# Graph attention stack on one core: outer products and aggregation of the last layer as one piece, in column tiles; one operation less in each norm

## The chip, the cores and the metric

The kernel runs on one core of a Trainium2 chip. It is a single program. The metric is the device time in microseconds (us) from the first to the last instruction; the time before is the median of three runs. A core has a matrix engine (TensorE, in the profile PE, its weight loads PEld), a vector engine (VectorE, DVE), an activation engine (ScalarE, ACT), a general engine (GpSimd, POOL) and a queue that starts transfers (SyncE, SP). Each has its own stream of instructions in fixed order, and they wait for one another through semaphores.

## The reference

There are 16 batches of 1024 nodes with 128 features. Three layers of masked attention with 8 heads and a feed-forward part come first; the fourth and last layer is a graph attention with one score per pair of nodes. All share one adjacency matrix.

```python
# layers 0 to 2
Q, K, V = h @ Wq, h @ Wk, h @ Wv                    # 8 heads of 16
scores  = where(adj == 0, -inf, Q K^T / sqrt(16))
attn    = softmax(scores) @ V
x = layer_norm(h + (attn @ Wo + bo))
x = layer_norm(x + relu(x @ W1 + b1) @ W2 + b2)

# layer 3, the last
h   = x @ W
e   = (h @ a_src)[:, :, None] + (h @ a_dst)[:, None, :]
e   = where(e >= 0, e, 0.2 * e)
e   = where(adj == 0, -inf, e)
att = softmax(e)
y   = einsum('bij,bjd->bid', att, h) + x
out = ln_gamma * (y - mean(y)) * rsqrt(var(y) + 1e-5) + ln_beta
```

In the last layer the exponential of a leaky sum of two terms is the larger of two products, one for each slope. So the kernel builds the numerators as outer products of two vectors, with no exponential per pair of nodes: TensorE forms a ratio as an outer product, VectorE takes the maximum with 1 and multiplies by the mask. The rest is in factors per node.

## The kernel before

The kernel is one long loop over score steps: 48 blocks (16 batches, 3 layers) of 32 steps. Each step makes scores for four heads (128 keys, 512 queries) on TensorE, exponentials and masks on the other three engines, and the weighted sum (attention times values) of the step that is four steps older. After the weighted sum of a step one *piece* of other work may be put in: a transpose, a projection, a part of the feed-forward layer, a part of the last layer. The pieces stand in chains, and a piece has a smallest distance in steps from the one before it.

```python
for at, (g, qh, kt) in enumerate(...):              # the steps of a block
    ...
    e = score_step(step)                            # L395 scores; L402, L403, L405, L417 on the other engines
    waiting.append((step, e, n + AHEAD))            # AHEAD = 4
    av_due(n)                                       # L422: weighted sum of an older step
    piece()                                         # at most one piece of other work
    n += 1

def piece():
    for chain in chains:
        if now[0] >= chain["due"] + chain["queue"][0][0] and take(chain):
            return
```

TensorE and ScalarE keep the order in which the program was written. The scores go to three pairs of banks of PSUM (`slot`), two in each step; all pieces share one bank (`bank`); tiles for the exponentials are six, and the outer products take from the same six.

```python
def slot(dtype=F32):
    return psum.tile([P, N], dtype, tag="s", name="s", bufs=3)
def bank():
    return psum.tile([P, 512], F32, tag="t", name="t", bufs=1)
def e_tile():
    return work.tile([P, J, 512], F32, tag="e", name="e", bufs=6)
```

A helper splits a matmul with 128 output rows into four, each with 32 columns of the weights and 32 output rows. The projections and the feed-forward part use it (L271):

```python
def by_columns(dst, lhsT, rhs, start=True, stop=True):
    for j in range(0, P, SLOT):                     # SLOT = 32
        nc.tensor.matmul(dst[j:j + SLOT, :], lhsT[:, j:j + SLOT], rhs, start=start, stop=stop)
```

The norms take mean and variance from VectorE and finish on GpSimd:

```python
def normalise(n, ts):
    z, _, mv = n
    m, v = mv[:, ts, 0], mv[:, ts, 1]
    nc.gpsimd.tensor_scalar(m, m, -1.0, None, op0=OP.mult)                   # L311
    nc.gpsimd.tensor_scalar(v, v, EPS, None, op0=OP.add)                     # L312
    nc.gpsimd.tensor_tensor(v, v, half_neg[:, ts], OP.pow)                   # L313
    for t in range(ts.start, ts.stop):
        nc.gpsimd.tensor_scalar(z[:, t, :], z[:, t, :], mv[:, t, 0:1], mv[:, t, 1:2], op0=OP.add, op1=OP.mult)   # L315
```

The last layer of a batch is a chain of pieces. A batch has four units of 256 queries; each unit has outer products and an aggregation:

```python
def nodes(t0, t1):                                  # projection of the nodes, L539
    ...
        nc.tensor.matmul(ps[:, (t - t0) * (D + 2):(t - t0 + 1) * (D + 2)],
                         s["xT", t // 4][:, t % 4 * P:(t % 4 + 1) * P], w_nodes, start=True, stop=True)
    ...
def edges(u):                                       # outer products of unit u
    e = s["e", u] = e_tile()...
    for c in range(2):
        ps = slot()
        ...  nc.tensor.matmul(ps[...], h_rows[...], g_rows[...], start=True, stop=True)          # L579, four
        nc.vector.scalar_tensor_tensor(e[:, c:NT:2, :], ps..., 1.0, mask01[...], op0=OP.max, op1=OP.mult)   # L582
def aggregate(u):
    e, ps = s["e", u], bank()
    for i in range(2):
        for t in range(NT):                         # NT = 8
            nc.tensor.matmul(ps[:, i * (D + 1):(i + 1) * (D + 1)], e[:, t, i * P:(i + 1) * P],
                             s["hd"][t // 4][:, t % 4, :], start=(t == 0), stop=(t == NT - 1))   # L591
    nc.vector.reciprocal(s["col"][:, 3, 2 * u:2 * u + 2], pv[:, :, D])                           # L594
    ...  # L597: times the reciprocal, plus x; then the statistics; a norm after every second unit

return [..., (2, rows_gh, ""), (8, edges(0), ""), (2, edges(1), ""), (1, aggregate(0), ""),
        (2, edges(2), ""), (1, aggregate(1), ""), (2, edges(3), ""), (1, aggregate(2), ""),
        (2, aggregate(3), ""), (4, end, "-x -last -w -w")]
```

The first number of an entry is the smallest distance in steps; the strings name tiles that the piece takes or gives back.

Of the kernel before, what the change touches and what calls it, by code (L numbers as in the profile page):

```python
# [15 lines left out]
OP = mybir.AluOpType  # L16
AX = mybir.AxisListType

P = 128
# [87 lines left out]
def fast_path(ctx: ExitStack, tc: tile.TileContext, a: dict, out: bass.AP, flag):  # L107
    nc = tc.nc
    x_dram, adj = a["x"], a["adj"]
    B, N, D = x_dram.shape  # L110
    NT = N // P
# [13 lines left out]
    def bank():  # L125

        return psum.tile([P, 512], F32, tag="t", name="t", bufs=1)
# [80 lines left out]
    w_nodes = const.tile([P, D + 2], F32)  # L208
# [36 lines left out]
    for i in range(2):  # L245
        t = const.tile([P, NT, H, HD + 1], F32, name=f"v{i}")
# [4 lines left out]
    def soon():  # L251

        return tc.high_priority(offset=SOON)
# [14 lines left out]
    def by_columns(dst, lhsT, rhs, start=True, stop=True):  # L268

        for j in range(0, P, SLOT):  # L270
            nc.tensor.matmul(dst[j:j + SLOT, :], lhsT[:, j:j + SLOT], rhs, start=start, stop=stop)  # L271
# [16 lines left out]
    def with_stats(x):  # L288

        return (x, work.tile([P, NT, 6], F32, tag="st", name="st", bufs=4),  # L290
                work.tile([P, NT, 2], F32, tag="mv", name="mv", bufs=4))
# [15 lines left out]
    def normalise(n, ts):  # L307

        z, _, mv = n
        m, v = mv[:, ts, 0], mv[:, ts, 1]  # L310
        nc.gpsimd.tensor_scalar(m, m, -1.0, None, op0=OP.mult)  # L311
        nc.gpsimd.tensor_scalar(v, v, EPS, None, op0=OP.add)  # L312
        nc.gpsimd.tensor_tensor(v, v, half_neg[:, ts], OP.pow)  # L313
        for t in range(ts.start, ts.stop):
            nc.gpsimd.tensor_scalar(z[:, t, :], z[:, t, :], mv[:, t, 0:1], mv[:, t, 1:2], op0=OP.add, op1=OP.mult)  # L315

    def scale_shift(z, gain, bias):
        n = z.shape[1]
        nc.gpsimd.tensor_mul(z, z, rows(gain, n))  # L319
        nc.gpsimd.tensor_add(z, z, rows(bias, n))  # L320
# [192 lines left out]
    def last_tasks(b):  # L513
        s = {}
        g0 = 32 * (b % 2)

        def xt(h):
            def run():
                w = W[L - 1]
                if h == 0:  # L520

                    s["col"] = work.tile([P, 4, NT], F32, tag="col", name="col", bufs=2)
                    s["hd"] = [work.tile([P, 4, D + 1], F32, tag="w", name="hd", bufs=TILES["w"]) for _ in range(2)]
                    s["n"] = with_stats(state["x", b])
                s["xT", h] = transpose_half("xT", state["x", b], h, w["ln2_gc"], w["ln2_bc"])
                if h == 1:
                    scale_shift(state["x", b], w["ln2_g"], ln2_b_last)
            return run

        def nodes(t0, t1):  # L530
            def run():
                col, ts = s["col"], slice(t0, t1)

                halves = [slice(max(t0, 4 * h), min(t1, 4 * h + 4)) for h in range(2)]
                halves = [(c, s["hd"][c.start // 4][:, c.start % 4:(c.stop - 1) % 4 + 1, :])
                          for c in halves if c.start < c.stop]
                ps = bank()
                for t in range(t0, t1):
                    nc.tensor.matmul(ps[:, (t - t0) * (D + 2):(t - t0 + 1) * (D + 2)],  # L539
                                     s["xT", t // 4][:, t % 4 * P:(t % 4 + 1) * P], w_nodes, start=True, stop=True)  # L540
                pv = ps[:, :(t1 - t0) * (D + 2)].rearrange("p (t d) -> p t d", d=D + 2)
                with soon():
                    nc.scalar.activation(col[:, 2, ts], pv[:, :, D + 1], AF.Exp, scale=NEG_SLOPE)
                    nc.scalar.activation(col[:, 0:2, ts].rearrange("p c t -> p t c"), pv[:, :, D:], AF.Exp,
                                         scale=1 - NEG_SLOPE)
                    for c, hd in halves:
                        nc.vector.tensor_mul(hd[:, :, :D], pv[:, c.start - t0:c.stop - t0, :D],
                                             col[:, 2, c, None].to_broadcast([P, c.stop - c.start, D]))
                for c, hd in halves:
                    nc.scalar.copy(hd[:, :, D], col[:, 2, c])  # L550
            return run

        def rows_gh():
            ps = bank()[:2 * NT, :P]
            nc.tensor.transpose(ps, s["col"][:, 0:2, :].rearrange("p c t -> p (c t)"), identf)
            parts = work.tile([2 * NT, 2, P], F32R, tag="parts", name="parts", bufs=1)
            with soon():
                nc.scalar.copy(parts[:, 0, :], ps)
                nc.vector.tensor_sub(parts[:, 1, :], ps, parts[:, 0, :].bitcast(F32))
            for r in range(2):  # L560

                queue = nc.scalar if r and b == B - 1 else nc.sync
                for i in range(4):
                    row = 64 * r + g0 + i
                    queue.dma_start(g_rows[row:row + 1, :].bitcast(F32), parts[:NT, i // 2, :].bitcast(F32))
                    queue.dma_start(h_rows[row:row + 1, :].bitcast(F32),
                                    parts[NT + 4 * r:NT + 4 * r + 4, i % 2, :].bitcast(F32))


        def edges(u):  # L570
            def run():
                e = s["e", u] = e_tile().rearrange("p j (c q) -> p (j c) q", q=256)
# [4 lines that stand above are left out]
                        for r in range(2):  # L577
                            row = slice(64 * r + g0, 64 * r + g0 + 4)
                            nc.tensor.matmul(ps[:, (2 * r + i) * 256:(2 * r + i + 1) * 256],  # L579
                                             h_rows[row, (2 * i + c) * P:(2 * i + c + 1) * P],  # L580
                                             g_rows[row, u * 256:(u + 1) * 256], start=True, stop=True)
                    nc.vector.scalar_tensor_tensor(e[:, c:NT:2, :], ps.rearrange("p (j q) -> p j q", q=256), 1.0,  # L582
                                                   mask01[:, c:NT:2, u * 256:(u + 1) * 256], op0=OP.max, op1=OP.mult)
            return run

        def aggregate(u):
            def run():
                e, ps = s["e", u], bank()
                for i in range(2):
                    for t in range(NT):  # L590
                        nc.tensor.matmul(ps[:, i * (D + 1):(i + 1) * (D + 1)], e[:, t, i * P:(i + 1) * P],  # L591
                                         s["hd"][t // 4][:, t % 4, :], start=(t == 0), stop=(t == NT - 1))
                pv = ps[:, :2 * (D + 1)].rearrange("p (i d) -> p i d", d=D + 1)
                nc.vector.reciprocal(s["col"][:, 3, 2 * u:2 * u + 2], pv[:, :, D])  # L594
                for i in range(2):
                    t = 2 * u + i
                    nc.vector.scalar_tensor_tensor(s["n"][0][:, t, :], pv[:, i, :D], s["col"][:, 3, t:t + 1],  # L597
                                                   state["x", b][:, t, :], op0=OP.mult, op1=OP.add)
                stats(s["n"], slice(2 * u, 2 * u + 2))
                if u % 2:  # L600
                    normalise(s["n"], slice(2 * u - 2, 2 * u + 2))
                if u == 3:
                    check_range(s["col"].rearrange("p c t -> p (c t)"))
            return run

        def end():
            y = s["n"][0]
            for h in range(2):
                scale_shift(y[:, 4 * h:4 * h + 4, :], wl["ln_gamma"], wl["ln_beta"])
                queue = nc.scalar if h and b == B - 1 else nc.sync  # L610
                queue.dma_start(out[b].rearrange("(t p) d -> p t d", p=P)[:, 4 * h:4 * h + 4], y[:, 4 * h:4 * h + 4, :])

        return [(5, xt(0), "+w +last +w +w"), (1, xt(1), "+w"), (2, nodes(0, 3), ""), (2, nodes(3, 6), ""), (2, nodes(6, 8), "-w -w"),
                (2, rows_gh, ""), (8, edges(0), ""), (2, edges(1), ""), (1, aggregate(0), ""),
                (2, edges(2), ""), (1, aggregate(1), ""), (2, edges(3), ""), (1, aggregate(2), ""),
                (2, aggregate(3), ""), (4, end, "-x -last -w -w")]

# [94 lines left out]
    with tc.manual_schedule(engines={mybir.EngineType.PE, mybir.EngineType.Activation}):  # L714
        for m, (b, l) in enumerate(blocks):
# [3 lines left out]
            for at, (g, qh, kt) in enumerate((g, qh, kt) for g, qh in order for kt in range(NT)):  # L719
# [18 lines left out]
                e = score_step(step)  # L738
# [23 lines left out]
    ps = bank()  # L762
# [226 lines left out]
```

## Time and profile before

| what | value |
|---|---|
| time, median of 3 runs | 4240.29 us (4239.9 to 4240.64) |
| profiled execution, span | 4233.0 us |
| TensorE busy | 3878.9 us (92%) |
| VectorE busy | 3405.0 us (80%) |
| ScalarE busy | 3396.3 us (80%) |
| GpSimd busy | 3449.9 us (82%) |
| scores L395 | 6144 matmul records, 1227.4 us busy |
| weighted sums L422 | 12288 matmul records, 1640.6 us busy |
| aggregation L591 | 2048 matmul records, 267.4 us busy |
| node projection L539 | 256 matmul records, 44.5 us busy |
| VectorE waiting for L591 | 185.7 us, 64 times |
| mean granted TensorE clock | 0.976 |

Busy time of an engine is the union of its instructions, and that of TensorE holds matmuls that overlap. A line of the groups reads: line, engine, operation, output <- input with shape, number; then busy time, mean duration in nanoseconds, and the idle time of that engine just before. A line of the chain that ended last names the piece of work that released the next; at its end it gives by engine 48% TensorE, 22% VectorE, 11% ScalarE, 9% GpSimd and 9% in which nothing shown was waited for. A float32 matmul leaves two records and two weight loads in the trace.

### The profile page before, as it was taken

How to read it: one execution, taken by the hardware profiler on the slowest of the kernel's cores; microseconds unless marked ns; L12 is line 12 of the kernel's file. 1: busy time of each engine (PE TensorE's matmuls, PEld its weight loads, DVE VectorE, ACT ScalarE, POOL GpSimd, SP SyncE). 2: the span in 40 equal slices, each digit the busy share in tenths (PEclk: the TensorE clock that was granted, in tenths of full speed). 3: DMA queues.
4: the chain of work that ended last, by engine and by line, in shares of the span. 5: the costliest groups of instructions: out<-in, count | busy, mean ns of one | idle time of the engine just before them, and what ended most of it. 6: DMA issues, size and time to landing. Idle time of an engine off the chain costs nothing.

```text
span 4233.0 us, 93837 instructions
## 1 busy us (share of the span) xinstructions
PE 3878.9 (92%) x37589; PEld 1582.0 (37%) x37589; DVE 3405.0 (80%) x5324; ACT 3396.3 (80%) x3961; POOL 3449.9 (82%) x3010
## 2 busy tenths in 40 slices
PE   7999999999988999999989999999998899999986
PEld 2333333344443333334444333333444433333445
DVE  6888888877768888888777888888877788888874
ACT  7899999976768999987766899997876689999760
POOL 5888888977769888888766988888886698888785
PEclk9999999999999999999999999999999999999998
DMA  5222122211111222121111212221211212212100
GB/s 150 64 61 61 49 53 61 61 51 51 44 51 49 61 61 61 49 53 51 51 51 51 61 50 52 61 61 43 70 48 36 64 42 61 58 49 57 46 22 17
DMA packets 126235, 232.23 MB, mean 55 GB/s; under 512 B 36704, under 2 KB 75616, under 8 KB 125792
## 3 DMA queue, kind: packets, MB, share of 16 engines
q1 hardware_dynamic: 122896, 225.14, 21.1%
q8 instruction: 299, 4.90, 0.5%
q10 hardware_dynamic: 2896, 1.01, 0.1%
q14 instruction: 144, 1.18, 0.1%
HBM read 15.54 MB, written 8.39 MB: 6 GB/s over the span
## 4 chain that ended last, share of the span: by engine, by line
PE 48%; DVE 22%; ACT 11%; POOL 9%; issue 9%; SPq 1%; DMA 1%; DVEq 0%; ACTq 0%; POOLq 0%
PE acc L422 15%; PE t L271 12%; PE s L395 11%; DVE e L405 11%; PE t L591 6%; POOL e L403 5%; ACT e L417 5%; ACT e L402 4%; DVE st L296 2%; PE t L260 2%; DVE e L582 2%; DVE lo L360 2%; DVE x L303 1%; POOL x L315 1%; DVE tt L433 1%
## 5 line engine op out<-in xcount | busy, mean ns | idle before, releaser
L405 DVE TENSOR_TENSOR e<-s,mask_add 128x1024 f32<-128x1024 f32 x2112 | 2501.3, 1212 | 427.0 <-PE s L395 307.1
L417 ACT ACTIVATE e<-e 128x1024 f32<-128x1024 f32 x2112 | 2196.3, 1063 | 387.4 <-DVE e L405 369.5
L403 POOL TENSOR_TENSOR e<-e,mask 128x1024 f32<-128x1024 f32 x960 | 2049.4, 2152 | 473.9 <-ACT e L402 469.7
L422 PE MATMUL acc<-e,v 128*17 128x512 f32 x12288 | 1640.6, 606 | 73.8 <-POOL e L403 40.9
L395 PE MATMUL s<-Wq,Wk 64*128 64x512 f32 x6144 | 1227.4, 462 | 114.4 <-DVE e L405 37.6
L402 ACT ACTIVATE e<-s 128x1024 f32<-128x1024 f32 x960 | 983.8, 1025 | 272.3 <-PE s L395 169.8
L395 PEld LDWEIGHTS s<-Wq,Wk 64*128 64x128 f32 x6144 | 504.8, 186 | 1087.1 <-DVE e L405 432.4
L422 PEld LDWEIGHTS acc<-e,v 128*17 128x17 f32 x12288 | 207.4, 95 | 584.9 <-issue 459.5
L315 POOL TENSOR_SCALAR x<-x,mv 128x128 f32<-128x128 f32 x896 | 392.1, 453 | 24.1
L591 PE MATMUL t<-hd,e 128*128 128x129 f32 x2048 | 267.4, 292 | 22.3 <-DVE lo L360 17.0
L591 PEld LDWEIGHTS t<-hd,e 128*128 128x128 f32 x2048 | 255.6, 206 | 81.9 <-issue 53.7
L319 POOL TENSOR_TENSOR x<-x,ln_g 128x1024 f32<-128x1024 f32 (+1 forms) x97 | 229.6, 2367 | 30.1 <-PE t L260 29.7
L313 POOL TENSOR_TENSOR mv<-mv,half_neg 128x4 f32<-128x4 f32 x224 | 232.3, 1037 | 18.3
L303 DVE TENSOR_TENSOR x<-t,x 128x512 f32<-128x512 f32 x192 | 131.8, 687 | 102.7 <-PE t L271 101.7
L271 PE MATMUL t<-x1T,W 128*32 128x512 f32 x1536 | 200.8, 594 | 3.4 <-DVE x L597 1.0
L296 DVE BATCH_NORM_STATS2 st<-x 128x6 f32<-128x128 f32 x896 | 196.8, 279 | 2.9
L271 PEld LDWEIGHTS t<-W,hT 128*32 128x32 f32 x6144 | 171.2, 110 | 70.5 <-issue 32.6
L271 PE MATMUL t<-W,hT 128*32 128x128 f32 x6144 | 186.3, 273 | 7.9 <-DVE x L303 3.7
L260 PE MATMUL t<-identf,x 128*128 128x128 f32 x896 | 149.6, 291 | 42.7 <-DVE lo L360 21.6
L260 PEld LDWEIGHTS t<-identf,x 128*128 128x128 f32 x896 | 96.3, 143 | 236.5 <-issue 89.5
L311 POOL TENSOR_SCALAR mv<-mv 128x4 f32<-128x4 f32 x224 | 53.0, 237 | 153.5 <-DVE mv L298 112.1
L594 DVE RECIPROCAL col<-t 128x2 f32<-128x2 f32 x64 | 10.9, 170 | 185.7 <-PE t L591 185.7
(83 smaller groups left out, 2634.3 us busy)
## 6 DMA issues: line engine op xcount, KB each, us to landing
Wk<-hi SPq DMA_DIRECT2D x384, 128.0 KB
Wk<-lo SPq DMA_DIRECT2D x384, 128.0 KB
Wq<-hi SPq DMA_DIRECT2D x384, 128.0 KB
Wq<-lo SPq DMA_DIRECT2D x384, 128.0 KB
x<-in_x_dram SPq DMA_DIRECT2D x16, 512.0 KB
out_dram<-x SPq DMA_DIRECT2D x31, 256.0 KB
ai<-in_adj_dram SPq DMA_DIRECT2D x8, 512.0 KB
g_rows<-parts SPq DMA_DIRECT2D x124, 4.0 KB
```

What stands on the lines that cost most here:

```text
L260: nc.tensor.transpose(ps[:, t * P:(t + 1) * P], src[:, 4 * h + t, :], identf)
L271: nc.tensor.matmul(dst[j:j + SLOT, :], lhsT[:, j:j + SLOT], rhs, start=start, stop=stop)
L296: nc.vector.bn_stats(st[:, t, :], z[:, t, :])
L313: nc.gpsimd.tensor_tensor(v, v, half_neg[:, ts], OP.pow)
L315: nc.gpsimd.tensor_scalar(z[:, t, :], z[:, t, :], mv[:, t, 0:1], mv[:, t, 1:2], op0=OP.add, op1=OP.mult)
L395: nc.tensor.matmul(ps[:, r * 512:(r + 1) * 512], k[64 * r:64 * r + 64, kt * P:(kt + 1) * P], q[64 * r:64 * r + 64, q0:q0 + 512], start=Tru ...
L402: nc.scalar.activation(ev, psv, AF.Exp, scale=HD ** -0.5)
L403: nc.gpsimd.tensor_mul(ev, ev, m)
L405: nc.vector.tensor_add(ev, psv, m)
L417: nc.scalar.activation(ev, ev, AF.Exp, scale=HD ** -0.5)
L422: nc.tensor.matmul(acc[j * SLOT:j * SLOT + HD + 1, :], v_bufs[m % 2][:, kt, 2 * j + g, :], e[:, j, :], start=first, stop=last)
L591: nc.tensor.matmul(ps[:, i * (D + 1):(i + 1) * (D + 1)], e[:, t, i * P:(i + 1) * P], s["hd"][t // 4][:, t % 4, :], start=(t == 0), stop=(t ...
```

## The change

It has three parts, all of which leave the computed function as it is. The outer products of unit u + 1 and the aggregation of unit u become one piece, with a distance of three steps to the next. The aggregation and the node projection are written with the helper for column tiles, four matmuls with 32 columns in place of one with 128; the weighted sums around them work in such tiles too. The norms no longer negate the mean before adding it, but subtract it. The aim is to spare TensorE a change of layout, to let VectorE work on the outer products while TensorE aggregates, and to relieve GpSimd.

```diff
     def normalise(n, ts):
 
         z, _, mv = n
-        m, v = mv[:, ts, 0], mv[:, ts, 1]
-        nc.gpsimd.tensor_scalar(m, m, -1.0, None, op0=OP.mult)
+        v = mv[:, ts, 1]
         nc.gpsimd.tensor_scalar(v, v, EPS, None, op0=OP.add)
         nc.gpsimd.tensor_tensor(v, v, half_neg[:, ts], OP.pow)
         for t in range(ts.start, ts.stop):
-            nc.gpsimd.tensor_scalar(z[:, t, :], z[:, t, :], mv[:, t, 0:1], mv[:, t, 1:2], op0=OP.add, op1=OP.mult)
+            nc.gpsimd.tensor_scalar(z[:, t, :], z[:, t, :], mv[:, t, 0:1], mv[:, t, 1:2], op0=OP.subtract, op1=OP.mult)
 ...
                 for t in range(t0, t1):
-                    nc.tensor.matmul(ps[:, (t - t0) * (D + 2):(t - t0 + 1) * (D + 2)],
-                                     s["xT", t // 4][:, t % 4 * P:(t % 4 + 1) * P], w_nodes, start=True, stop=True)
+                    by_columns(ps[:, (t - t0) * (D + 2):(t - t0 + 1) * (D + 2)],
+                               s["xT", t // 4][:, t % 4 * P:(t % 4 + 1) * P], w_nodes)
 ...
                     for t in range(NT):
-                        nc.tensor.matmul(ps[:, i * (D + 1):(i + 1) * (D + 1)], e[:, t, i * P:(i + 1) * P],
-                                         s["hd"][t // 4][:, t % 4, :], start=(t == 0), stop=(t == NT - 1))
+                        by_columns(ps[:, i * (D + 1):(i + 1) * (D + 1)], e[:, t, i * P:(i + 1) * P],
+                                   s["hd"][t // 4][:, t % 4, :], start=(t == 0), stop=(t == NT - 1))
 ...
+        def two(f, g):
+            def run():
+                f()
+                g()
+            return run
+
         return [...
-                (2, rows_gh, ""), (8, edges(0), ""), (2, edges(1), ""), (1, aggregate(0), ""),
-                (2, edges(2), ""), (1, aggregate(1), ""), (2, edges(3), ""), (1, aggregate(2), ""),
-                (2, aggregate(3), ""), (4, end, "-x -last -w -w")]
+                (2, rows_gh, ""), (8, edges(0), ""), (3, two(edges(1), aggregate(0)), ""),
+                (3, two(edges(2), aggregate(1)), ""), (3, two(edges(3), aggregate(2)), ""),
+                (3, aggregate(3), ""), (4, end, "-x -last -w -w")]
```

## The prediction

> **What bounds the kernel now.** I read the table of engines first: TensorE 92% busy, the other three 80 to 82%. No engine is at its limit over the whole span, and overlapping matmuls are counted as busy, so 92% says little. Next came the busy time by stretch, which shows that the span alternates between two stages:
>
> ```profile
> core 0: us, PE busy (x) PEld busy (x) DVE busy (x) ACT busy (x) POOL busy (x), PEclk, DMA share, GB/s
> 1270.00:1850.00 580.00, 541.71 (x5528) 196.96 (x5526) 491.93 (x752) 519.11 (x591) 518.83 (x449) 1.00 0.23 57
> 1850.00:2320.00 470.00, 431.09 (x3948) 197.71 (x3944) 360.84 (x588) 331.07 (x402) 347.76 (x303) 0.95 0.19 50
> ```
>
> The first row has no last layer in it: ScalarE and GpSimd are busy 89% of it. The second has the last layer of four batches, and ScalarE falls to 70%, GpSimd to 74%. All that the change touches on TensorE is in such stages, where the other engines wait. Who waits is in the timeline of one unit (outer products L579, then aggregation L591), first TensorE; start and duration in us lead each line, the wait before it stands in brackets:
>
> ```profile
> 859.43 1.05 PE L422 MATMUL acc<-e,v 128*17 128x512 f32 x8
> 860.41 0.50 PE L579 MATMUL s<-g_rows,h_rows 4*128 4x256 f32 x4
> 861.33 0.50 PE L579 MATMUL s<-g_rows,h_rows 4*128 4x256 f32 x4 [0.41 <-DVE e L405]
> 861.75 0.49 PE L395 MATMUL s<-Wq,Wk 64*128 64x512 f32 x2
> 862.46 0.50 PE L395 MATMUL s<-Wq,Wk 64*128 64x512 f32 x2 [0.21 <-DVE e L582]
> 862.89 1.05 PE L422 MATMUL acc<-e,v 128*17 128x512 f32 x8
> 863.87 3.84 PE L591 MATMUL t<-hd,e 128*128 128x129 f32 x32
> 867.64 0.73 PE L395 MATMUL s<-Wq,Wk 64*128 64x512 f32 x4
> 868.30 1.05 PE L422 MATMUL acc<-e,v 128*17 128x512 f32 x8
> ```
>
> The same stretch on VectorE:
>
> ```profile
> 861.19 2.35 DVE L582 SCALAR_TENSOR_TENSOR e<-s,mask 128x1024 f32<-128x1024 f32 x2
> 864.08 1.23 DVE L405 TENSOR_TENSOR e<-s,mask_add 128x1024 f32<-128x1024 f32 x1 [0.55 <-PE acc L422]
> 867.75 0.17 DVE L594 RECIPROCAL col<-t 128x2 f32<-128x2 f32 x1 [2.44 <-PE t L591]
> ```
>
> A step of the pipeline goes from one L422 to the next. The step with the outer products takes 3.46 us here, the one with the aggregation 5.41. In the first, TensorE waits for VectorE to empty the score banks; in the second, VectorE waits 2.44 us for the aggregation. The chain that ended last follows the same turns:
>
> ```profile
> 861.19 1.23 DVE e L582
> 862.41 0.04 issue
> 862.46 0.50 PE s L395 x2
> 862.96 0.98 PE acc L422 x8
> 863.94 3.78 PE t L591 x32
> ```
>
> So outer product, score step and aggregation stand one after the other in the time. I measured all steps of the timeline in this way: 491 with nothing between take 1.92 us in the mean, 55 with outer products 3.94, 54 with an aggregation 6.23; together 941 + 217 + 336 = 1,495 us. The other steps carry projections or transposes, and the last ten aggregations lie in the tail after the last score.
>
> [...]from the start of an L422 group, which works in column tiles, to a full-array group takes 0.98 us (862.89 to 863.87), to another group in column tiles 0.87 us (4086.95 to 4087.82). [...]a 32-record group in column tiles goes from 512.55 to the next group at 513.56 (1.01 us), a 64-record one from 4087.82 to 4089.68 (1.86 us), so 26.6 ns for each further record. [...] The stage with the last layer has a mean clock of 0.95 and the other 1.00, and several aggregations take 5.2 to 5.7 us in place of 3.84. [...]here an operation on 4 elements per partition takes 237 ns.
>
> **The change part by part.**
>
> Aggregation in column tiles. The page counts 32 records for 16 matmuls, two for each. Now there are 64 matmuls, so 128 records: 1.86 + 64 x 0.0266 = 3.56 us to the next group, where the full array takes 3.77 (863.87 to 867.64). With 0.11 us less for entering, an aggregation saves 0.32 us. Four tiles side by side do not make it four times as fast[...]. This is an estimate from groups with 128 moving columns, here it is 129.
>
> One piece instead of two. The order of the two built programs on TensorE gives: 42 steps with both (outer products of the next unit, then the aggregation of this one), 14 with outer products alone, 13 with an aggregation alone, and 529 empty in place of 490 (the timeline shows one more). The combined step, from the lines above: first outer products at +0.98, second at +1.90 (still behind L405), +0.42 until the next group can start, 3.56 for the aggregation, 0.66 for the scores: 6.5 us. VectorE's 2.35 us on the outer products now lie beside the aggregation, and its wait shrinks from 2.44 to about 1.8 us (861.19 + 2.35 = 863.54, against 859.43 + 5.9 = 865.3). But the two steps measured are dearer in the mean than the clean case: 3.94 - 3.46 = 0.5 and 6.23 - 5.41 = 0.8. [...] I give the combined step half of this 1.3: 7.2 us. The sum: 42 x 7.2 + 14 x 3.94 + 13 x 5.9 + 529 x 1.92 = 302 + 55 + 77 + 1,016 = 1,450, or 45 us less. With none of the excess it would be 73 less, with all of it 18.
>
> Node projections in column tiles. Six full records go from 4057.09 to 4057.96 (0.87 us); 24 records in tiles are 0.19 + 24 x 0.0266 = 0.83, and 0.11 for entering: 0.15 us saved, with four records 0.13. For 28 and 14 steps: 6 us.
>
> Norms. The negation on GpSimd goes, 224 times:
>
> ```profile
> L311 POOL TENSOR_SCALAR mv<-mv 128x4 f32<-128x4 f32 x224 | 53.0, 237 | 153.5 <-DVE mv L298 112.1
> ```
>
> The wait for the statistics in the last column stays and passes to the next operation. What goes is 53 us busy and the gap to that operation (15.1 us over all), 68 us of GpSimd. The subtract has the same form as the add. GpSimd carries 9% of the chain that ended last, so I count 6 us.
>
> Tail. Ten aggregations at 0.2, and four norms on the last chain at 0.3: 3 us.
>
> Given back. After a combined step two outer-product tiles are held out of six, so the next scores write into a tile that is free only after the weighted sum of their own step. Before, the aggregation stood there and hid this; now about 0.15 us of a step shows, 42 times: 6 us.
>
> Sum: 45 + 6 + 6 + 3 - 6 = 54 us, so 4240 - 54 = 4186 us, 1.3% less.
>
> **The rivals.** First: the combined piece starves the others. No score comes for some 6.5 us, where before there were scores between the two long pieces; ScalarE has about 2 us of work in hand and then stands. If the empty steps after it then run at the pace of ScalarE (two activations of 1.05 us, 2.1 us a step) instead of 1.92, the 84 steps that follow combined ones lose 15 us, and the result is about 4200. For it: ScalarE and GpSimd already wait 3 us beside an aggregation. Against it: they have 26 to 30% to spare in this stage.
>
> Second: column tiles are no gain. If the 64 pairs of loads and matmuls for aggregation take 30 ns a record and not 26.6, each takes 0.4 us more, and 64 of them turn the saving of 20 us into nothing: about 4206. The weights are slices of 32 columns, as in the projections, which speaks for 26.6.
>
> Third: [...] Then the excess of 1.3 us is nearly all saved and more elsewhere: 4155. Speaking for it are the slow groups just after a wait (at 850 us an L422 group of 1.91 us for 1.05). Against: the other half of the waits stays.
>
> Fourth: the moved pieces meet projections of the next block at other places, and the waits for the single projection bank (17 us before aggregations, behind the lo split) come or go. That is worth 10 us to either side.
>
> **Range and chances.** The rivals span 4155 to 4206, and the fourth shifts each; I take 4152 to 4222. Over 2% faster means below 4155.5, which needs nearly all the excess saved: 0.13. Over 2% slower means over 4325; nothing in the sum comes near it: 0.02. Within 2%: 0.85.
>
> **What would show it right or wrong.** In the changed profile the aggregation group has 8,192 records and goes 3.5 to 3.6 us to the next group; the combined steps take 6.5 to 7.5 us; VectorE's reciprocal waits in all less than 140 us (185.7 now); the clock of the stages with the last layer is 0.95 or above; GpSimd is busy some 53 us less. A record pace of 30 ns, empty steps well over 2 us, or stages without the last layer that change by more than 5 us each would prove the sum wrong.

## The result and the profile after

The changed kernel takes 4236.49 us (median of 4 runs, 4234.09 to 4238.0), the kernel before 4240.09 beside it. The ratio is 0.9992, with a 95% interval of 0.9975 to 1.0009: no measurable change. The prediction was 4186 us with a range of 4152 to 4222, so the result lies outside it.

The page of the profile after, first its table of engines, then the sums by engine of the chain that ended last, then two groups of instructions:

```profile
PE 3816.1 (90%) x44501; PEld 1544.2 (36%) x44501; DVE 3405.5 (80%) x5324; ACT 3412.0 (81%) x3961; POOL 3698.5 (87%) x2786
...
POOL 43%; PE 38%; DVE 10%; ACT 4%; issue 4%; DMA 1%; SPq 1%; ACTq 0%; DVEq 0%; POOLq 0%
...
L421 PE MATMUL acc<-e,v 128*17 128x512 f32 x12288 | 1633.9, 604 | 195.9 <-POOL e L402 152.5
...
L314 POOL TENSOR_SCALAR x<-x,mv 128x128 f32<-128x128 f32 x896 | 700.8, 795 | 22.9
```

The same two groups in the page of before:

```profile
L422 PE MATMUL acc<-e,v 128*17 128x512 f32 x12288 | 1640.6, 606 | 73.8 <-POOL e L403 40.9
L315 POOL TENSOR_SCALAR x<-x,mv 128x128 f32<-128x128 f32 x896 | 392.1, 453 | 24.1
```

From the norm on, every line number is one lower than before, because the negation is gone (L315 is now L314, L422 is L421). The number to see is 795 ns for the last operation of the norm. Before, the same 896 operations on the same shape took 453 ns and 392.1 us together; now 700.8. GpSimd should have lost 53 us and has gained 249 (3449.9 to 3698.5), and it carries 43% of the chain that ended last instead of 9%. TensorE's weighted sums now wait 152.5 us for GpSimd's masked exponentials; before it was 40.9.

The busy time by stretch, same stretches and columns as in the prediction (PE, PEld, DVE, ACT, POOL, then clock, DMA share, GB/s):

```profile
1270.00:1850.00 580.00, 523.29 (x5298) 188.49 (x5298) 473.81 (x703) 508.71 (x568) 528.43 (x390) 0.99 0.21 54
1850.00:2320.00 470.00, 431.32 (x5863) 196.26 (x5860) 379.35 (x628) 350.04 (x430) 406.92 (x314) 0.98 0.22 56
```

In the first stretch, which holds no last layer, GpSimd is now the busiest engine but for TensorE (528 of 580 us), and TensorE gets 18 us less done than before. In the second, with the last layer, GpSimd goes from 348 to 407 us busy, and the clock from 0.95 to 0.98.

A combined step in the timeline of TensorE, laid out as in the prediction:

```profile
882.03 1.05 PE L421 MATMUL acc<-e,v 128*17 128x512 f32 x8
883.02 0.50 PE L578 MATMUL s<-g_rows,h_rows 4*128 4x256 f32 x4
883.73 0.50 PE L578 MATMUL s<-g_rows,h_rows 4*128 4x256 f32 x4 [0.20 <-ACT e L401]
884.15 3.76 PE L271 MATMUL t<-hd,e 128*32 128x129 f32 x128
887.84 0.73 PE L394 MATMUL s<-Wq,Wk 64*128 64x512 f32 x4
888.50 1.05 PE L421 MATMUL acc<-e,v 128*17 128x512 f32 x8
```

The same on VectorE:

```profile
883.64 2.36 DVE L581 SCALAR_TENSOR_TENSOR e<-s,mask 128x1024 f32<-128x1024 f32 x2 [0.17 <-PE s L578]
887.98 0.17 DVE L593 RECIPROCAL col<-t 128x2 f32<-128x2 f32 x1 [1.98 <-PE t L271]
```

The step takes 6.47 us (882.03 to 888.50), the 6.5 of the prediction's working. VectorE's 2.36 us on the outer products (883.64 to 886.00) lie, but for the first 0.5 us, beside the aggregation (884.15 to 887.84). The aggregation, 8192 records in all and 128 here, takes 3.69 us to the next group, not the 3.56 of the prediction.

I measured the time from each weighted sum to the next in the whole timeline, sorted by what lies between, and also the time of every stage of 128 steps:

| | before | after |
|---|---|---|
| steps with nothing between | 491 x 1.92 | 531 x 1.98 |
| steps with outer products alone | 55 x 3.93 | 14 x 3.81 |
| steps with an aggregation alone | 54 x 6.23 | 13 x 5.28 |
| combined steps | none | 42 x 6.22 |
| sum of these | 1494.7 us | 1433.5 us |
| transposes L260, 216 steps | 2.60 each | 2.73 each |
| query projection Wq, 94 steps | 2.64 each | 3.13 each |
| a stage without the last layer | 304.5 to 304.7 us | 313.7 us |
| a layer 2 with the layer 0 after it, which hold the last layer | 737.5 to 740.1 us | 721.2 to 724.2 us |

So the combined piece and the tiles brought more than predicted: 61 us less in these steps for 45, even with empty steps that had become slower. The stages in which the change touches the norms alone lost 9 us each.

**Theory N** (theory A in the expectations below). The form of the operation decides its duration on GpSimd: subtract then multiply takes some 795 ns where add then multiply takes 453, and this eats the gain. **Rival to it** (theory B there). The combined piece or the tiles make GpSimd slower, by traffic or by bunching its work, and give their gain back. A second question follows: where does the piece's gain come from, if it exceeds what I gave it?

### The profile page after: what moved, and what is told of

The parts are those of the page before. It is cut to its first block, busy times and chain, and to the rows that moved or that the text cites. A ratio compares the mean times of both kernels' runs of the same rounds, so it can differ in the third digit from the quotient of the medians.

```text
span 4234.7 us, 107443 instructions
## 1 busy us (share of the span) xinstructions
PE 3816.1 (90%) x44501; PEld 1544.2 (36%) x44501; DVE 3405.5 (80%) x5324; ACT 3412.0 (81%) x3961; POOL 3698.5 (87%) x2786
## 4 chain that ended last, share of the span: by engine, by line
POOL 43%; PE 38%; DVE 10%; ACT 4%; issue 4%; DMA 1%; SPq 1%; ACTq 0%; DVEq 0%; POOLq 0%
POOL e L402 20%; PE t L271 15%; PE acc L421 12%; POOL x L314 12%; PE s L394 9%; DVE e L404 5%; POOL mv L312 4%; POOL x L318 2%; ACT e L401 2%; POOL x L319 2%; PE t L260 2%; ACT e L416 1%; DVE st L296 1%; POOL A L435 1%; POOL mv L311 1%
## 5 line engine op out<-in xcount | busy, mean ns | idle before, releaser
L421 PE MATMUL acc<-e,v 128*17 128x512 f32 x12288 | 1633.9, 604 | 195.9 <-POOL e L402 152.5
L394 PE MATMUL s<-Wq,Wk 64*128 64x512 f32 x6144 | 1193.5, 457 | 72.3 <-ACT e L401 27.9
L394 PEld LDWEIGHTS s<-Wq,Wk 64*128 64x128 f32 x6144 | 492.8, 186 | 1042.8 <-issue 486.1
L314 POOL TENSOR_SCALAR x<-x,mv 128x128 f32<-128x128 f32 x896 | 700.8, 795 | 22.9
L421 PEld LDWEIGHTS acc<-e,v 128*17 128x17 f32 x12288 | 208.1, 95 | 731.8 <-issue 384.7
L271 PE MATMUL t<-hd,e 128*32 128x129 f32 x8192 | 244.8, 276 | 7.1 <-DVE x L596 3.2
L318 POOL TENSOR_TENSOR x<-x,ln_g 128x1024 f32<-128x1024 f32 x97 | 229.4, 2365 | 12.7 <-PE t L260 12.6
L271 PEld LDWEIGHTS t<-hd,e 128*32 128x32 f32 x8192 | 226.7, 111 | 26.8 <-issue 5.3
L260 PE MATMUL t<-identf,x 128*128 128x128 f32 x896 | 155.0, 298 | 39.6 <-DVE x L303 12.6
L260 PEld LDWEIGHTS t<-identf,x 128*128 128x128 f32 x896 | 99.1, 146 | 236.5 <-issue 78.4
L581 DVE SCALAR_TENSOR_TENSOR e<-s,mask 128x1024 f32<-128x1024 f32 x128 | 150.5, 1210 | 5.9 <-PE s L578 5.0
```

The costliest lines, as they stand in the source:

```text
L260: nc.tensor.transpose(ps[:, t * P:(t + 1) * P], src[:, 4 * h + t, :], identf)
L394: nc.tensor.matmul(ps[:, r * 512:(r + 1) * 512], k[64 * r:64 * r + 64, kt * P:(kt + 1) * P], q[64 * r:64 * r + 64, q0:q0 + 512], start=Tru ...
L421: nc.tensor.matmul(acc[j * SLOT:j * SLOT + HD + 1, :], v_bufs[m % 2][:, kt, 2 * j + g, :], e[:, j, :], start=first, stop=last)
```

## The experiments

**Each part alone.** Four kernels divide the change. The kernel before was at 4238.23 us beside them. The first is the changed kernel with the old norm:

```diff
-        v = mv[:, ts, 1]
+        m, v = mv[:, ts, 0], mv[:, ts, 1]
+        nc.gpsimd.tensor_scalar(m, m, -1.0, None, op0=OP.mult)
...
-    nc.gpsimd.tensor_scalar(z[:, t, :], z[:, t, :], mv[:, t, 0:1], mv[:, t, 1:2], op0=OP.subtract, op1=OP.mult)
+    nc.gpsimd.tensor_scalar(z[:, t, :], z[:, t, :], mv[:, t, 0:1], mv[:, t, 1:2], op0=OP.add, op1=OP.mult)
```

> The changed kernel with the norm of before (negate the mean, then add and multiply); pieces and column tiles stay. Theory A: the subtract form of the norm costs 795 ns on GpSimd where the add form costs 453, 896 times, and this makes GpSimd the bound and eats what pieces and tiles save. Then the norm operation is back at 453 ns, a stage of 128 steps without the last layer is back at about 305 and 344 us (now 314 and 353), the stages with the last layer stay near 370, and the time is 4145 us (4125 to 4165). Theory B: the norm is innocent, and the combined piece moves other work so that the gain of the last layer is given back elsewhere: the time stays at 4230 to 4250.

Measured: 4122.53 us, ratio 0.9723 (0.9707 to 0.974), 2.5 us below the expected range and far from theory B. Page of this kernel, sum of the chain by engine and the norm's group:

```profile
PE 47%; DVE 19%; ACT 12%; POOL 12%; issue 9%; SPq 1%; DMA 1%; DVEq 0%; ACTq 0%; POOLq 0%
...
L315 POOL TENSOR_SCALAR x<-x,mv 128x128 f32<-128x128 f32 x896 | 389.2, 448 | 24.0
```

The operation is back at 448 ns with piece and tiles in place, GpSimd is down to 12% of the chain, and the stages without the last layer are back at 304.5 to 304.8 us. Simply putting the negation back makes the kernel 114 us quicker than the changed one. This is the fastest version of the study, 2.8% below the kernel before.

The second is the kernel before with the new norm alone:

```diff
-        nc.gpsimd.tensor_scalar(m, m, -1.0, None, op0=OP.mult)
...
-    ..., op0=OP.add, op1=OP.mult)
+    ..., op0=OP.subtract, op1=OP.mult)
```

> The kernel before with the subtracting norm alone. Theory A: 896 operations of 795 ns for 453, less 53 us for the negation, are 250 us more of GpSimd; the nine stages without the last layer grow by some 9 us each, and those with it a little: 4320 us (4300 to 4340). Theory B: one operation less, 4234 us.

Measured: 4393.82 us, ratio 1.0367 (1.035 to 1.0384). The norm's group in its page, where GpSimd carries 44% of the chain:

```profile
L314 POOL TENSOR_SCALAR x<-x,mv 128x128 f32<-128x128 f32 x896 | 701.0, 796 | 22.9
```

Neither piece nor tiles are there, and the operation takes 796 ns: theory N stands, its rival falls. The part alone costs 156 us, nearly twice the 82 expected. The 896 operations take 309 us more; half of this comes out as time.

The third is the kernel before with column tiles alone (node projection and aggregation with `by_columns`, two pieces as before; the diff of the change shows the edit):

> The kernel before with column tiles in aggregation and node projection alone. By the prediction's sum for the tiles (0.32 us for each of 64 aggregations, 6 us for nodes, 3 in the tail) 4210 us. If pace per record were 30 ns and tiles no gain: 4240. Theory A says nothing against either; GpSimd is as before.

Measured: 4227.53 us, ratio 0.9976 (0.9968 to 0.9983), or 10.7 us less, between the two times expected (4210 and 4240). The fourth is the kernel before with the combined piece alone, in full-array matmuls:

```diff
-   (2, edges(1), ""), (1, aggregate(0), ""), (2, edges(2), ""), ...
+   (3, two(edges(1), aggregate(0)), ""), (3, two(edges(2), aggregate(1)), ""), ...
```

> The kernel before with outer products and aggregation as one piece alone, full array, add norm. Theory A, with some 90 us saved by pieces and tiles together and 30 of them from tiles: 4180 us. Theory B, the combined piece gives back elsewhere what it saves: 4230 to 4250.

Measured: 4130.94 us, ratio 0.9739 (0.9723 to 0.9755), or 107 us less, and 49 below the 4180 expected. The aggregation group in its page:

```profile
L591 PE MATMUL t<-hd,e 128*128 128x129 f32 x2048 | 247.0, 278 | 5.0 <-DVE x L597 3.1
```

Before, this group was busy 267.4 us and TensorE stood 22.3 us ahead of it, 17 of them for the projection bank behind the lo split. Now it is 247.0 and 5.0. In the timeline of before, 16 of the 54 aggregations ahead of the tail take over 4.2 us, at granted clocks of 0.68 to 0.90, where the others take 3.81 to 3.85 at 1.00; here none of 55 takes over 4.2. The stages without the last layer stand at 304.5 to 304.7, as before; the three pairs of stages with it lose 30 to 33 us each, and the tail after the last weighted sum 10 (106.8 to 96.5).

The three parts add up to -107.3 - 10.7 + 155.6 = +37.6 us, and together they make -3.6. The subtract costs 156 us in the kernel before and 114 on top of the other two; why less there is not shown. Only the tiles add up with the piece: 4130.94 against 4122.53, 8 us.

**Is it the subtract, or the place of it?** A bench ahead of the kernel's first stage: eight operations of each form on one tile of the norm's shape. The rest is the first experiment's kernel.

```diff
+    for _ in range(8):
+        nc.gpsimd.tensor_scalar(bz, bz, bs[:, 0:1], bs[:, 1:2], op0=OP.add, op1=OP.mult)
+    ...                       # subtract, mult; then mult, add; mult, subtract; add; subtract; last on VectorE
```

> Pieces, tiles and add norm, and ahead of everything, on a tile of its own (128 x 128, all ones), eight operations each of six forms on GpSimd and one on VectorE, all with two scalars per partition or one. Theory A (the form costs, wherever its data come from): add then multiply 450 ns, subtract then multiply 795. If it is the subtract itself: multiply then subtract and the plain subtract are slow as well, multiply then add and the plain add near 450. Theory C (the place costs: the statistics as scalars, strides): all forms alike near 450 on the tile of ones. VectorE: some 200 ns. The time of the whole is longer by the bench and says nothing.

The view of this tile, one line for each form: instructions, then shortest, median and longest duration in ns, and the stretch in us:

```profile
L169 POOL TENSOR_SCALAR bz<-bz,bs x8: 451/452/863, 2.5 to 19.2; 128x128 f32<-128x128 f32 x8
L171 POOL TENSOR_SCALAR bz<-bz,bs x8: 795/798/1344, 20.0 to 30.4; 128x128 f32<-128x128 f32 x8
L173 POOL TENSOR_SCALAR bz<-bz,bs x8: 452/454/454, 31.3 to 35.2; 128x128 f32<-128x128 f32 x8
L175 POOL TENSOR_SCALAR bz<-bz,bs x8: 795/796/806, 35.7 to 42.0; 128x128 f32<-128x128 f32 x8
L177 POOL TENSOR_SCALAR bz<-bz,bs x8: 604/606/621, 42.9 to 47.8; 128x128 f32<-128x128 f32 x8
L179 POOL TENSOR_SCALAR bz<-bz,bs x8: 604/605/609, 48.5 to 53.4; 128x128 f32<-128x128 f32 x8
L181 DVE TENSOR_SCALAR bz<-bz,bs x8: 338/346/348, 54.0 to 57.8; 128x128 f32<-128x128 f32 x8
```

In order: add-multiply 452, subtract-multiply 798, multiply-add 454, multiply-subtract 796, add alone 606, subtract alone 605, and subtract-multiply on VectorE 346, not the 200 expected, which was a guess that no view had shown. From 27.2 to 54.0 us VectorE does nothing at all, so the forms from L173 to L179 ran without it: 454 against 796 is the form, not traffic. A subtract by itself costs no more than an add (605 and 606 ns). Only in a pair does it cost some 344 ns more, in either position. And the pair add-multiply is quicker than its add alone.

**Can the work leave GpSimd?** In the first experiment's kernel, the negation moves to VectorE:

```diff
-        nc.gpsimd.tensor_scalar(m, m, -1.0, None, op0=OP.mult)
+        nc.vector.tensor_scalar(m, m, -1.0, None, op0=OP.mult)
```

> Pieces, tiles and add norm, with the negation of the mean on VectorE. 53 us less on GpSimd, some 30 more on VectorE, which wait for one another in any case: 4122 us as without it (4110 to 4135).

Measured: 4137.79 us, ratio 0.9762 (0.9745 to 0.9778), 15 us slower than with the negation on GpSimd and above the expected range. All instructions of that line, as for the bench:

```profile
L311 DVE TENSOR_SCALAR mv<-mv x224: 115/160/2124, 124.7 to 4129.8; 128x4 f32<-128x4 f32 x112
```

Four numbers per partition take 160 ns in the middle and up to 2124; the mean is 421, against 237 on GpSimd. In the changed kernel I then moved the whole subtract-multiply to VectorE, which does it in 346 ns by the bench:

```diff
-    nc.gpsimd.tensor_scalar(z[:, t, :], z[:, t, :], ..., op0=OP.subtract, op1=OP.mult)
+    nc.vector.tensor_scalar(z[:, t, :], z[:, t, :], ..., op0=OP.subtract, op1=OP.mult)
```

> The changed kernel with the subtract-and-multiply of the norm on VectorE, all 896, where the subtract is one operation of some 200 ns. GpSimd loses 701 us of its 3699, VectorE gains some 180. If GpSimd is what binds the changed kernel (theory A) this is much below 4236, and at or below the 4122 of the add form: 4110 us (4070 to 4160). Theory B would leave it at 4236.

Measured: 4980.57 us, ratio 1.1753 (1.1733 to 1.1772). The expectation missed by 870 us. Timeline of VectorE in that kernel, four of the operations in one line:

```profile
313.85 7.22 DVE L314 TENSOR_SCALAR x<-x,mv 128x128 f32<-128x128 f32 x4 [0.37 <-POOL mv L312]
```

The same stretch on GpSimd:

```profile
314.12 2.14 POOL L402 TENSOR_TENSOR e<-e,mask 128x1024 f32<-128x1024 f32 x1 [0.31 <-ACT e L401]
316.23 2.34 POOL L318 TENSOR_TENSOR x<-x,ln_g 128x1024 f32<-128x1024 f32 x1
318.65 2.34 POOL L319 TENSOR_TENSOR x<-x,bo 128x1024 f32<-128x1024 f32 x1
```

Four operations of 341 ns take 7.22 us, from just before the first of these GpSimd operations starts to the time at which the third ends (313.85 + 7.22 = 321.07, and 318.65 + 2.34 = 320.99). VectorE gets about one of them done per GpSimd operation. All 896 of the line:

```profile
L314 DVE TENSOR_SCALAR x<-x,mv x896: 327/341/2499, 124.0 to 4971.6; 128x128 f32<-128x128 f32 x180
```

The median is 341 ns, not the 200 guessed, the longest 2499, and the mean 838. By the trace, 619 of the 896 have no GpSimd operation beside them (by more than 0.05 us) and take 327 to 350 ns; the other 277 take 1954 in the mean. VectorE is busy 4089.1 us, and GpSimd's 3014.4, 684 less than in the changed kernel, bring nothing. So in this kernel VectorE's operation is held up beside one of GpSimd: 341 ns becomes up to 2499, about one GpSimd operation (2.14 or 2.34 us above) and its own time. Why, no run here shows. I had looked at the busy shares alone.

A second bench tests this, and which pairs are quick:

```diff
+    for _ in range(6):
+        nc.gpsimd.tensor_scalar(bz, bz, bs[:, 0:1], bs[:, 1:2], op0=OP.mult, op1=OP.mult)
+    ...                       # max, mult; then mult alone; by is a tile of ones that GpSimd does not touch
+    for _ in range(16):
+        nc.gpsimd.tensor_mul(bv, bv, bv)                                       # 128x1088
+    for _ in range(6):
+        nc.vector.tensor_scalar(by, by, bs[:, 0:1], bs[:, 1:2], op0=OP.subtract, op1=OP.mult)
+    for _ in range(6):
+        nc.vector.scalar_tensor_tensor(by, by, bs[:, 0:1], bs[:, 1:2].to_broadcast([P, D]), op0=OP.mult, op1=OP.mult)
+    ...                       # the same two forms again, on bz
```

> Pieces, tiles and add norm, and ahead of the loop again operations on tiles of ones. First on GpSimd, 128 x 128: multiply-multiply, maximum-multiply, multiply alone, while it also runs products of 128 x 1088 (about 2.3 us each). If only the pair of one add and one multiply has the quick form: 795, 795 and 605 ns; if the subtract were the slow part: 450 for multiply-multiply. On VectorE, beside the long products of GpSimd, six subtract-multiply operations and six operations of the form with a second tensor, then the same alone. If VectorE's operation stands still while a GpSimd operation runs (as the 838 ns in the mean in the kernel with the norm on VectorE suggest): 2 us and more for one beside the products, 341 alone. If it does not: 341 in both places. The time of the whole says nothing.

The two lines beside the products, whose 16 operations take 2.0 us each:

```profile
L266 DVE TENSOR_SCALAR by<-by,bs x6: 330/364/2168, 16.0 to 24.7; 128x128 f32<-128x128 f32 x6
L268 DVE SCALAR_TENSOR_TENSOR by<-by,bs x6: 334/401/1482, 25.6 to 34.1; 128x128 f32<-128x128 f32 x6
```

The view of the other tile: GpSimd's three forms in the order of the edit, then VectorE:

```profile
L255 POOL TENSOR_SCALAR bz<-bz,bs x6: 448/454/975, 5.4 to 18.4; 128x128 f32<-128x128 f32 x6
L257 POOL TENSOR_SCALAR bz<-bz,bs x6: 793/1277/1884, 20.8 to 37.2; 128x128 f32<-128x128 f32 x6
L259 POOL TENSOR_SCALAR bz<-bz,bs x6: 596/602/608, 40.4 to 52.0; 128x128 f32<-128x128 f32 x6
L270 DVE TENSOR_SCALAR bz<-bz,bs x6: 347/347/4210, 52.6 to 58.4; 128x128 f32<-128x128 f32 x6
L272 DVE SCALAR_TENSOR_TENSOR bz<-bz,bs x6: 350/352/352, 58.8 to 60.7; 128x128 f32<-128x128 f32 x6
```

And what GpSimd runs when L270 begins, two operations of the kernel itself:

```profile
52.54 4.20 POOL L427 TENSOR_TENSOR e<-e,mask 128x1024 f32<-128x1024 f32 x2
```

Multiply-multiply takes 454 ns, as add-multiply; I had expected 795 if only the latter was quick, so the quick form is wider than one pair. Max-multiply takes 793 at its shortest; its longer ones fall where VectorE works beside it. Both VectorE forms can be held up (2168 and 1482 ns at the longest beside the products). In the trace, each of the five operations over 500 ns ends some 0.1 us after a long GpSimd operation has ended. Three stand beside products of the bench (2168, 2036 and 1482 ns), one beside the end of such a product (883 ns). The longest is the first of L270, 4210 ns from 52.60: it ends at 56.81, and the two GpSimd operations at 56.74. The other five of L270, with nothing on GpSimd, take 347 ns. Not every operation is held up: several took some 330 ns while GpSimd was at one of its max-multiply pairs, and those pairs then took 793 to 1884 ns.

**Why the piece brings 107 us.** The prediction has the outer products' 2.35 us on VectorE beside the aggregation (R1). The rival (R2) is that it is enough to have both in one step, whatever the order: one step less with its waits, and the bank asked for at another place. The experiment is the fourth kernel with the two calls swapped, so that the aggregation comes first and VectorE has nothing to do beside it:

```diff
-   (3, two(edges(1), aggregate(0)), ""), ...
+   (3, two(aggregate(0), edges(1)), ""), ...
```

> One piece, full array, add norm, with the aggregation ahead of the outer products. Theory R1 (the gain of the piece comes from VectorE's work on the outer products lying beside the aggregation): a combined step takes 0.98 + 3.77 + 0.5 and then waits for VectorE before the second scores, about 7.4 us for 6.3; 42 such steps give 45 us back: 4176. Theory R2 (the gain comes from one interruption less of the score steps, with its waits and slow clock): 4131 as in the other order.

Measured: 4249.78 us, ratio 1.0028 (1.0018 to 1.0038), 119 us more than in the other order. R2 falls. R1 named the side but not the size: it had 4176. A combined step on TensorE in this kernel:

```profile
863.23 1.05 PE L422 MATMUL acc<-e,v 128*17 128x512 f32 x8
864.21 3.84 PE L591 MATMUL t<-hd,e 128*128 128x129 f32 x32
867.98 0.73 PE L579 MATMUL s<-g_rows,h_rows 4*128 4x256 f32 x8
868.65 0.50 PE L395 MATMUL s<-Wq,Wk 64*128 64x512 f32 x2
870.54 0.60 PE L395 MATMUL s<-Wq,Wk 64*128 64x512 f32 x2 [1.39 <-DVE e L582]
871.07 1.91 PE L422 MATMUL acc<-e,v 128*17 128x512 f32 x8
```

VectorE's next operation after the aggregation:

```profile
868.09 0.17 DVE L594 RECIPROCAL col<-t 128x2 f32<-128x2 f32 x1 [3.42 <-PE t L591]
```

VectorE stands 3.42 us while TensorE aggregates, and then TensorE stands 1.39 us while VectorE empties the outer products. The next weighted sum then takes 1.91 us, not 1.05. In the kernel before, the first of these two windows holds a weighted sum of 1.91 us (from 850.21), the second one of 1.05 (from 857.11); the columns are those of the prediction:

```profile
850.21:852.05 1.84, 1.84 (x10) 0.15 (x9) 0.55 (x1) 0.00 (x0) 0.00 (x0) 0.50 0.00 0
857.11:858.09 0.98, 0.98 (x10) 0.13 (x9) 0.98 (x5) 0.00 (x0) 0.00 (x0) 1.00 0.00 0
```

The granted clock was 0.50 in the first and 1.00 in the second. With the same 1.91 us the slow group of the swapped order fits a clock of 0.50; that is an estimate from these two. What lowers the clock, no run shows. Over the whole timeline, 45 groups of weighted sums take over 1.2 us here, 23 in the fourth kernel. The combined step takes 7.76 us in the mean, against 6.30 in the fourth kernel: 42 x 1.46 = 61 us. The steps with the feed-forward and key projections take about 39 more, which I did not follow, and the tail, 129.2 us against 96.5, 33 more. These make 133; the profiled spans differ by 127 (4256.3 against 4129.1).

In the tail no score step stands between two pieces. From aggregation to aggregation there, first in the fourth kernel:

```profile
4088.55 3.81 PE L591 MATMUL t<-hd,e 128*128 128x129 f32 x32 [0.33 <-DVE x L597]
4092.29 0.73 PE L579 MATMUL s<-g_rows,h_rows 4*128 4x256 f32 x8
4093.36 3.81 PE L591 MATMUL t<-hd,e 128*128 128x129 f32 x32 [0.33 <-DVE x L597]
```

Then with the order swapped:

```profile
4215.32 0.49 PE L591 MATMUL t<-hd,e 128*128 128x129 f32 x2 [1.89 <-DVE e L582]
4216.52 6.56 PE L591 MATMUL t<-hd,e 128*128 128x129 f32 x30 [0.71 <-DVE e L582]
4223.01 0.74 PE L579 MATMUL s<-g_rows,h_rows 4*128 4x256 f32 x8
4225.57 0.49 PE L591 MATMUL t<-hd,e 128*128 128x129 f32 x2 [1.82 <-DVE e L582]
```

One unit takes 4.81 us in the first and 10.25 in the second, where the aggregation waits for VectorE to empty the outer products made just before it, and then runs slowly, 6.56 us. From the tail's first outer products to the end of its last aggregation this makes 43.7 us in the fourth kernel and 72.5 with the order swapped, 29 of the 33. The order also decides ahead of the tail: the last weighted sum starts at 4126.2 us before the change, at 4032.7 in the fourth kernel and at 4127.1 with the order swapped.

## Why the prediction was wrong

| step of the prediction | predicted, us | measured, us |
|---|---|---|
| piece: 45 in the steps, of which 54 x 0.32 = 17 are the tiles', and 6 given back | 22 less | 107 less alone |
| tiles: these 17, 6 in the nodes, 2 in the tail | 25 less | 8 to 11 less |
| norms: 6, and 1 in the tail | 7 less | 114 more on top of the others, 156 more alone |
| sum | 54 less | 3.6 less |

**Norms: the step that failed.** "The subtract has the same form as the add." It has not. The view had a duration for add-multiply, 453 ns, and I carried it over to an operation which no row of that profile held. The instruction is of the same kind with the same shape; the arithmetic in it differs, and with it the time is 795 ns. With 896 of them this is 309 us more busy time on an engine that had 18% of slack over the span and 11% in the stages without the last layer. The prediction itself had given "stages without the last layer that change by more than 5 us each" as the sign that the sum is wrong. They change by 9.

**The combined step: right in its working, wrong in the allowance.** The clean case was worked out at 6.5 us; the steps measured take 6.21 in the first experiment's kernel, and 6.22 in the changed one. "I give the combined step half of this 1.3" added 0.65 us that is not there: with the clean case too high as well, 42 x (7.2 - 6.21) = 42 us. The lone aggregations take 5.28 us, not 5.9, which is 8 more; the empty steps (531 of them, not 529) are 4 in all below the sum's 1,016; the 14 lone outer products 1. With the 45 of the prediction this makes 100, and that kernel's timeline has 99.5 less in these steps. The waits that go are seen (for the bank behind the lo split, 17 us before, and for the score banks, in the swapped order), and so are fewer groups of weighted sums over 1.2 us (23 against 37 before, where their granted clocks are 0.50 to 0.83). The third rival said that nearly all of the excess goes, 4155 us. It was given too little weight, and the gain goes further than I had put it. Overlap and clock can't be told apart fully: the first experiment's kernel has both the overlap and a higher mean granted clock (0.985 against 0.976 before), and the swapped order lost both at once (0.971).

**Wait of the reciprocal: right.** Predicted less than 140 us in all:

```profile
L593 DVE RECIPROCAL col<-t 128x2 f32<-128x2 f32 x64 | 10.8, 169 | 92.7 <-PE t L271 92.7
```

It is 92.7, from 185.7. The piece alone gives 91.1 and the tiles alone 180.7, so it is the piece that does this.

**Tiles: mis-sized.** The pace of 26.6 ns a record came from 64-record groups with 128 moving columns; with 128 records and 129 columns it is (3.69 - 1.86) / 64 = 28.6 ns, so an aggregation takes 3.69 us and not 3.56. The second rival named 30 ns, and 4206 us for it. The lone aggregation step drops from 5.44 us with the piece in full matmuls to 5.28 in tiles, 0.16 us in place of 0.32. Entering saves the 0.11 us predicted (0.98 to 0.87 in the middle of these steps); the aggregation itself saves 0.08 (3.77 to 3.69) where 0.21 was in the sum. What the tiles bring in all, 8 to 11 us, is under half of their 25.

**Given back, and starvation (first rival): not seen, and hardly tested.** Both are costs of the steps just after a combined one, and the first rival reckoned with 84 empty ones. In the first experiment's kernel only 5 of these steps are empty; the rest carry other pieces. Empty steps as a whole take 1.91 us there. The 1.98 of the changed kernel comes from the norms, since the old norm takes it away with piece and tiles kept, and the new norm alone gives 2.00.

**The range** was built from rivals on TensorE, VectorE and ScalarE; the norms had no rival, because 7 us seemed too little for one. Without the subtract the result would have missed the range too, on the other side: 4122.53 against a lower end of 4152.

## What to carry to other kernels

A duration from a profile holds for the operation in it, not for its kind: when a change swaps the arithmetic inside an instruction on GpSimd, measure the new pair (here 795 ns for 453), and multiply by how often it runs. When two long pieces go into one step, try first the order in which the one that feeds another engine comes first: here it gained 107 us, and the same two calls in the other order lost the whole gain (4131 against 4250 us). And before work moves from GpSimd to VectorE, look at the longest duration of its instructions there, not at the busy shares: 4122 us became 4138 with a four-element operation moved, and moving the 896 norms of the changed kernel brought it from 4236 to 4981.

## What was not expected of the hardware

On GpSimd, at 128x128 in float32, pairs of add and multiply take 452 to 454 ns, pairs with a subtract 796 to 798, max-multiply 793 at its shortest, and one add, subtract or multiply alone 602 to 606. So a pair can be quicker than its half; the runs show that the form decides, and not why. On VectorE the subtract-multiply pair takes 346 ns when nothing runs on GpSimd (first bench), up to 2499 in the kernel with the norm on VectorE, and 4210 behind two GpSimd operations (second bench).
